# A graph layer's gather kernel: a first block without filled places, its list loaded first, and the fillers' columns computed with one partition for each step

## The chip, the cores and the metric

The kernel runs on one core of a Trainium2 chip. The metric is device time in microseconds (us), the median of three runs. Engine names follow the profile: PE is the matrix engine, PEld its weight load, DVE the vector engine, ACT the scalar engine, POOL the GpSimd engine, SP the engine that here only issues transfers. A name with a q behind it (SPq, ACTq, POOLq) is that engine's issuing side.

## The reference, cut to what matters

There are 50,000 nodes with 128 features and 1,650,000 edges, sorted by the node that they go to. Every edge carries a type, 0 or 1, which chooses one of two weight matrices.

```python
Xs  = X[src]
msg = where(edge_type == 0, Xs @ W_data.T + b_data, Xs @ W_control.T + b_control)
agg = segment_sum(msg, dst, num_segments=50000)
y   = relu(agg + X @ W_self.T + b_self)
out = layernorm(X + y)          # over the 128 features
```

The kernel uses that the sum over edges and the product with the weights can change places: it first sums the rows `X[src]` of all edges of one type that go to one node, and multiplies the sums afterwards.

## The kernel before, in words

**Blocks, chunks and steps.** The edges are cut, in their order, into 438 blocks (`NBLK`) of `BE` = 3768. A block has four steps (`Q`). A step has seven chunks (`R`) of 128 edges, and 22 fillers (`F`) behind them; after the four steps come 96 single edges (`X`). So a block has 28 chunks in its list, 88 fillers and 96 single edges. Each chunk is one indirect gather, issued by POOL at line 408: a list of 128 node numbers on the partitions brings in 128 rows of `x` as a tile `y`. There are 70 such tiles (`gat`, `bufs=70`). PE multiplies each `y` by a one-hot matrix `oh` (line 411), which puts every row into the column of its node and type. One step's nodes span at most 36 columns (`W`) for each type.

**Filled places.** Some edges in the list go from a node to itself. Their rows need no gather, because the window of `x` that a block works on is loaded anyway. `fill(b)` takes such a place in the list of chunks and puts a filler's source there instead: the number of the place among its partition's free places (`rk`) is compared with 0 to 21 (line 273), the filler's packed value is picked (lines 276 to 285) and the place's list entry `idx` comes out at line 284. The self edges that were put out are added in another way: `left_out_columns`, `left_out_matrix`, `left_out_numbers`, `left_out_rows`, `add_left_out` (lines 292 to 329). The last block has no fillers; its list comes straight from the loaded edges.

**Groups.** Ten blocks are a group (`GB`); there are 44. `load_edges(g)` brings a group's sources, targets and types on the SP queue: `s`, `d`, `t` for the chunks (128 partitions x 290 numbers, 145 KB each), and `sf`, `df`, `tf` for the fillers, where all 880 numbers of the group are copied to each of the 128 partitions (440 KB each). `columns(g)` turns them into what `fill` and `onehot` need: `col`, `rk`, `cb`, `stay` for the chunks, and `v_f`, the packed value of every filler. Both halves go through the same helpers, `columns_of`, `check` and `packed` (lines 188 to 206), and a name with `_f` marks the fillers' half. `columns(g)` is called by `fill` for the first block of a group, and `fill` runs five blocks ahead (`RAHEAD`), so that it comes in step 2 of the sixth block of the group before; `load_edges(g + 1)` is called at the second block of a group.

**Single edges.** The 96 single rows of a block are brought by plain transfers of one row each, 48 on the SP queue and 48 on the ACT queue (line 396), two blocks ahead.

**Order.** The main part stands in a hand-written order. Ahead of the loop it does `fill` for five blocks with all of the chunks' and fillers' columns, `onehot` and `counts` for two, then the windows of `x` for three and the single rows of two. In the loop, block `b` has four turns, one for each step: `products` (the gathers and matrix products), `layer` and `moments` and `store` for the block before, `onehot` and `counts` for block `b + 2`, `fill` for block `b + 5`. What stands ahead of the hand-written part (constants, the loading and transposing of the weights in a pool `wts` that is closed before the pool `keep` is opened, the load of `first_i` at line 125, `base` and `begin` at lines 127 to 135) is interleaved by the framework.

## Time and profile before

| what | value |
|---|---|
| median of three runs | 15436.6 us (15436.29 to 15437.57) |
| the profiled execution's own time | 15434.21 us |
| its span, first to last instruction | 15432.5 us |
| busy: PE / PEld / DVE / ACT / POOL | 62% / 48% / 46% / 2% / 75% |
| gathers, POOL, line 408 | 12,236 from `idx` and 27 from `s`, mean 948 ns |
| DMA moved | 1009 MB, mean 65 GB/s |

The page gives each engine's busy share, the chain of work that ended last, and the costliest groups of instructions. The view of waits says for each engine and line whom it waited for, in total, how often and the longest. The timeline lists single instructions: start in us, duration in us, engine, line, operation, output and inputs, and in brackets the idle time ahead of it with the releaser. The groups by form separate shapes: output, inputs, count, then total busy us and mean ns of one.

### The profile page before, as it was taken

What the parts mean: (1) busy time and instruction counts of PE and PEld (TensorE: products, weight loads), DVE (VectorE), ACT (ScalarE), POOL (GpSimd) and SP (SyncE); (2) the same over time, 40 slices, a digit from 0 to 9 for tenths busy, and PEclk for the clock granted to TensorE, in tenths of its full rate; (3) what the DMA queues carried; (4) which work ended last, traced back from release to release, by engine and by line L of the source; (5) the groups of instructions that cost most, each with busy time, mean ns of one, the idle gap of its engine ahead of it and who ended that gap; (6) DMA issues with size and microseconds to landing.
All of it is one profiled execution on the core that took longest, in us unless ns stands there. A gap on an engine that the chain in (4) does not pass through costs nothing.

```text
span 15432.5 us, 254222 instructions
## 1 busy us (share of the span) xinstructions
PE 9551.6 (62%) x34515; PEld 7418.5 (48%) x34516; DVE 7169.3 (46%) x12518; ACT 355.9 (2%) x881; POOL 11631.9 (75%) x12273
## 2 busy tenths in 40 slices
PE   5666666666666666666666666666666666666666
PEld 4444444444444444444444444444444444444444
DVE  5444444444444444444444444444444444444442
ACT  0000000000000000000000000000000000000000
POOL 6777777777777777777777777777777777777777
DMA  2222222222222222222222222222222222222221
GB/s 67 65 65 69 65 65 65 64 65 65 65 65 67 68 65 65 65 65 65 65 65 65 70 65 65 65 65 65 65 65 65 65 70 65 65 65 65 65 65 57
DMA packets 705933, 1008.97 MB, mean 65 GB/s; under 512 B 263521, under 2 KB 490948, under 8 KB 704222
## 3 DMA queue, kind: packets, MB, share of 16 engines
q0 software_dynamic: 392416, 804.42, 18.3%
q1 hardware_dynamic: 269416, 177.18, 4.0%
q10 hardware_dynamic: 42390, 11.02, 0.3%
q14 instruction: 1426, 11.68, 0.2%
q8 instruction: 285, 4.67, 0.1%
HBM read 962.86 MB, written 28.70 MB: 64 GB/s over the span
## 4 chain that ended last, share of the span: by engine, by line
DMA 69%; issue 11%; POOL 10%; PE 7%; DVE 2%; POOLq 0%; SPq 0%; ACTq 0%; DVEq 0%; ACT 0%
DMA y<-in_x,idx 68%; POOL y L408 10%; PE acc L411 4%; PE po L435 1%; PE po L433 1%; PE po L432 0%; POOLq L408 0%; DMA yx<-in_x 0%; SPq L396 0%; ACTq L396 0%; DVE by L292 0%; PE acc L414 0%; DMA y<-in_x,s 0%; DVE stats L198 0%; DVE stats L199 0%
## 5 line engine op out<-in xcount | busy, mean ns | idle before, releaser
L408 POOL DMA_INDIRECT y<-in_x,idx x12236 | 11605.0, 948 | 3760.9 <-DMA y<-in_x,idx 1973.1
L411 PE MATMUL acc<-oh,y 128*128 128x72 f32 x24526 | 8011.2, 446 | 5293.3 <-DMA y<-in_x,idx 5204.0
L411 PEld LDWEIGHTS acc<-oh,y 128*128 128x128 f32 x24526 | 6050.7, 315 | 7176.0 <-DMA y<-in_x,idx 6659.5
L422 DVE TENSOR_TENSOR sums<-acc,sums 128x108 f32 x1752 | 473.5, 270 | 4399.2 <-PE acc L414 4321.4
L370 DVE TENSOR_REDUCE cnt<-oh 128x216 bf16<-128x1512 f32 x438 | 1238.3, 2827 | 0.1
L360 DVE TENSOR_TENSOR oh<-col,small 128x2088 f32<-128x2088 f32 x438 | 1005.8, 2296 | 0.0
L329 DVE TENSOR_TENSOR sums<-pl,sums 128x384 f32<-128x384 f32 x437 | 243.5, 557 | 1522.8 <-ACT sums L427 1522.8
L414 PEld LDWEIGHTS <-to_row 128*128 128x128 bf16 x3504 | 639.0, 198 | 0.1
L292 DVE TENSOR_REDUCE by<-old 128x88 bf16<-128x616 f32 x437 | 583.2, 1335 | 15.1
L306 DVE COPY at<-small 88x1 f32<-88x1 f32 x437 | 67.5, 154 | 1097.9 <-PE small L299 1083.9
L440 DVE SCALAR_TENSOR_TENSOR h<-po,xw 128x128 f32<-128x128 f32 x438 | 127.5, 291 | 939.1 <-PE po L435 929.7
L435 PE MATMUL po<-wmsgT,sums 128*128 128x128 f32 x1752 | 535.3, 461 | 0.0
L375 DVE TENSOR_REDUCE cnt<-oh 128x72 bf16<-128x576 f32 x438 | 512.7, 1170 | 0.0
L427 ACT COPY sums<-sums 128x384 f32 x437 | 223.9, 512 | 12101.5 <-DMA yx<-in_x 8363.0
L414 PE MATMUL acc<-cnt,to_row 128*128 128x36 bf16 x3504 | 468.9, 217 | 0.0
L435 PEld LDWEIGHTS po<-wmsgT,sums 128*128 128x128 f32 x1752 | 406.1, 322 | 98.3 <-issue 98.3
L299 PE MATMUL small<-ones_b,by 128*88 128x1 bf16 x437 | 94.1, 215 | 493.6 <-DVE by L292 493.6
L276 DVE TENSOR_TENSOR new<-m,small 128x616 f32<-128x616 f32 x437 | 347.5, 795 | 14.9
L273 DVE TENSOR_TENSOR m<-rk,small 128x616 f32<-128x616 f32 x437 | 347.5, 795 | 14.8
L280 DVE TENSOR_REDUCE v_new<-new 128x28 f32<-128x616 f32 x437 | 347.3, 795 | 14.9
L433 PE MATMUL po<-bias,sums 3*128 3x128 f32 x876 | 346.9, 497 | 0.0
L289 DVE TENSOR_TENSOR old<-m,small 128x616 f32<-128x616 f32 x437 | 343.5, 786 | 0.1
(110 smaller groups left out, 3996.0 us busy)
## 6 DMA issues: line engine op xcount, KB each, us to landing
yx<-in_x ACTq DMA_DIRECT2D x20976, 0.5 KB
yx<-in_x SPq DMA_DIRECT2D x20976, 0.5 KB
y<-in_x,idx POOLq DMA_INDIRECT x12236
xw<-in_x SPq DMA_DIRECT2D x438, 64.0 KB
xT<-in_x_t SPq DMA_DIRECT2D x438, 64.0 KB
out<-o SPq DMA_DIRECT2D x438, 64.0 KB
sf<-in_src_f SPq DMA_DIRECT2D x44, 440.0 KB
df<-in_dst_f SPq DMA_DIRECT2D x44, 440.0 KB
```

Source lines behind the costliest of these rows:

```text
L273: nc.vector.tensor_tensor(m, rk_g[g][:, i, :, None].to_broadcast([P, C, F]), rank_no_ps[:, None, :].to_broadcast([P, C, F]), op=ALU.is_equal)
L276: nc.vector.tensor_tensor(new.rearrange("p (q r) f -> p q r f", r=R), m.rearrange("p (q r) f -> p q r f", r=R), vf.rearrange("p (q f) -> p ...
L292: nc.vector.tensor_reduce(by, old.rearrange("p (q r) f -> p q f r", r=R), AX.X, ALU.add)
L360: nc.vector.tensor_tensor(oh[:, :n, :], col_g[g][:, i, :n, None].to_broadcast([P, n, 2 * W]), num_ps[:, None, :].to_broadcast([P, n, 2 * W ...
L370: nc.vector.tensor_reduce(cnt[:, :n, :], ohs[b][:, :n * R, :].rearrange("p (q r) w -> p q w r", r=R), AX.X, ALU.add)
L375: nc.vector.tensor_reduce(cnt[:, q, :], ohs[b][:, k[0]:k[-1] + 1, :].rearrange("p r w -> p w r"), AX.X, ALU.add)
L408: nc.gpsimd.indirect_dma_start(out=y[:r], out_offset=None, in_=x, in_offset=bass.IndirectOffsetOnAxis(ap=idxs[b][:r, k:k + 1], axis=0))
L411: nc.tensor.matmul(acc[:, :2, :].rearrange("p t w -> p (t w)"), y[:r], ohs[b][:r, k, :], start=k == ks[0], stop=k == ks[-1])
L414: nc.tensor.matmul(acc[:, 2, :], to_row[:, t, :], cnts[b][:, q, t * W:(t + 1) * W], start=t == 0, stop=t == 1)
L422: nc.vector.tensor_tensor(part, accs.pop((b, q)), part, op=ALU.add)
L433: nc.tensor.matmul(po, a[0:3, 2, :B], bias, start=False, stop=False)
L435: nc.tensor.matmul(po, a[:, t, :B], c["wmsgT"][:, t * D:(t + 1) * D], start=False, stop=t == 1)
```

## The change

**Block 0 is plain.** It gets 28 chunks of 128 edges and neither fillers nor single edges, like the last block. `plain(b)` is true for the first and the last block; `fill`, the five `left_out` functions and `single_rows` skip them. Its list is a tile of its own, `idx0`, 128 x 28 numbers, loaded on the SP queue ahead of the first `load_edges`. The number of blocks stays 438; the last block gets 28 chunks (3568 edges) in place of 27 (3384).

**The fillers' half on the partitions of its steps.** `sf`, `df`, `tf` become tiles of 40 x 22: one partition for each of the group's 40 steps, one column for each filler, loaded as they lie. The fillers' `rel`, `col`, `chk`, `lim` and `v` are 40 x 22 too, with their start `begin_p` computed once for all groups from a small load `first_p`. The result, 880 numbers, is written to a DRAM tile (`spread_out`) and read back to all 128 partitions (`spread_in`, tile `vf_all`, 440 KB), both on the SP queue.

**The order.** `load_edges(g + 1)` moves to the first block of a group, `columns(g + 1)` out of `fill` to step 2 of the third block, ahead of `left_out_rows`; `spread_out(g + 1)` and `spread_in(g + 1)` stand at the heads of the fourth and fifth. Ahead of the loop come the columns of group 0, the two transfers, the windows, `onehot` and `counts` of block 0, and then blocks 1 to 4 one after another.

```diff
-NBLK = -(-E // BE)
-REST = E - (NBLK - 1) * BE
+NBLK = 2 + (E - C * CH) // BE
+REST = E - C * CH - (NBLK - 2) * BE
...
+GS = GB * Q
+def plain(b):
+    return b == 0 or b >= NBLK - 1
...
+    nc.vector.memset(stats, 0.0)
...
         for name, a in (("sf", src_f), ("df", dst_f), ("tf", etype_f)):
-            t = eds.tile([P, GB, Q, F], I32, name=name, bufs=1)
-            nc.sync.dma_start(t.rearrange("p b q f -> p (b q f)"),
-                              row_bcast(a[g * GB * Q * F:(g + 1) * GB * Q * F]))
+            t = eds.tile([GS, F], I32, name=name, bufs=1)
+            nc.sync.dma_start(t, a[g * GS:(g + 1) * GS, :])
...
+    idx0 = keep.tile([P, C], I32, name="idx0")
+    nc.sync.dma_start(idx0, src_t[:, :C])
     load_edges(0)
...
+    two_p = keep.tile([GS, 2, GROUPS], I32, name="two_p")
+    nc.sync.dma_start(two_p, first_p.rearrange("s (m g) -> s m g", m=2))
+    base_p = keep.tile([GS, GROUPS], F32, name="base_p")
+    nc.vector.tensor_scalar(base_p, two_p[:, 1, :], 0.0, float(N - B), op0=ALU.max, op1=ALU.min)
+    begin_p = keep.tile([GS, GROUPS], F32, name="begin_p")
+    nc.vector.tensor_tensor(begin_p, two_p[:, 0, :], base_p, op=ALU.subtract)
+    nc.vector.tensor_scalar(begin_p, begin_p, 0.0, float(B - W), op0=ALU.max, op1=ALU.min)
+    nc.vector.tensor_tensor(begin_p, begin_p, base_p, op=ALU.add)
...
-            yield rel, d, first[:, :, :, None].to_broadcast([P, GB, Q, F])
+            yield rel, d, begin_p[:, g:g + 1].to_broadcast([GS, F])
...
+    def spread_out(g):
+        vd_g[g] = dram.tile([GS * F], F32, name="vd")
+        nc.sync.dma_start(vd_g[g].rearrange("(s f) -> s f", f=F), vp_g.pop(g))
+    def spread_in(g):
+        v = eds.tile([P, GB, Q, F], F32, name="vf_all")
+        nc.sync.dma_start(v.rearrange("p b q f -> p (b q f)"), row_bcast(vd_g.pop(g)))
+        v_g[g] = v
     def fill(b):
+        if plain(b):
+            return
         g, i = divmod(b, GB)
-        if i == 0:
-            columns(g)
...
-        nc.vector.tensor_copy(vf, v_f[:, i].rearrange("p q f -> p (q f)"))
+        nc.vector.tensor_copy(vf, v_g[g][:, i].rearrange("p q f -> p (q f)"))
...
-        n = C1 if b < NBLK - 1 else RCH if b < NBLK else 0
+        n = C1 if not plain(b) else C if b == 0 else RCH if b < NBLK else 0
...
-    idxs, bys, pcs, zs, pls = {}, {}, {}, {}, {}
+    idxs = {0: idx0}
+    bys, pcs, zs, pls = {}, {}, {}, {}
...
     with tc.manual_schedule():
-        for b in range(RAHEAD):
+        columns(0)
+        spread_out(0)
+        spread_in(0)
+        for b in range(3):
+            window(b)
+        onehot(0)
+        counts(0)
+        for b in range(1, RAHEAD):
             fill(b)
             left_out_columns(b)
             left_out_matrix(b)
-        for b in range(AHEAD):
-            onehot(b)
-            counts(b)
-        for b in range(3):
-            window(b)
-        for b in range(AHEAD):
-            for q in range(Q):
-                single_rows(b, q)
-        left_out_numbers(0)
-        left_out_rows(0)
+            if b < AHEAD:
+                onehot(b)
+                counts(b)
+                for q in range(Q):
+                    single_rows(b, q)
         for b in range(NBLK + 1):
             if b + 3 < NBLK:
                 window(b + 3)
             g, i = divmod(b, GB)
-            if i == 1 and g + 1 < GROUPS:
+            if i == 0 and g + 1 < GROUPS:
                 load_edges(g + 1)
+            if i == 3 and g + 1 < GROUPS:
+                spread_out(g + 1)
+            if i == 4 and g + 1 < GROUPS:
+                spread_in(g + 1)
...
+                if q == 2 and i == 2 and g + 1 < GROUPS:
+                    columns(g + 1)
                 if q == 2:
                     left_out_rows(b + 1)
                     if b + RAHEAD < NBLK:
                         fill(b + RAHEAD)
...
-                if b + AHEAD < NBLK - 1:
+                if not plain(b + AHEAD):
                     single_rows(b + AHEAD, q)
```

The host's layout of the edge lists follows these shapes.

More of the change, by code (lines that the diff above doesn't have):

```diff
@@ L65, with straight @@
 TBL = GROUPS * GB
+GS = GB * Q
+def plain(b):
+    return b == 0 or b >= NBLK - 1
 def row_bcast(ap, n=P):
     return bass.AP(tensor=ap.tensor, offset=ap.offset, ap=[[0, n], *ap.ap])
-def straight(ctx, tc, c, x, x_t, src_t, dst_t, etype_t, src_f, dst_f, etype_f, src_x, dst_first, out):
+def straight(ctx, tc, c, x, x_t, src_t, dst_t, etype_t, src_f, dst_f, etype_f, src_x, dst_first, first_p, out):
     nc = tc.nc
@@ L88, in straight @@
     keep_ps = ctx.enter_context(tc.tile_pool(name="keep_ps", bufs=1, space=bass.MemoryType.PSUM))
+    dram = ctx.enter_context(tc.tile_pool(name="vdram", bufs=2, space=bass.MemoryType.DRAM))
     eds = ctx.enter_context(tc.tile_pool(name="eds", bufs=2))
@@ L99, in straight @@
     loads = {}
-    col_g, rk_g, v_g, cb_g, one_g = {}, {}, {}, {}, {}
+    col_g, rk_g, stay_g, v_g, cb_g, vp_g, vd_g = {}, {}, {}, {}, {}, {}, {}
     stats = keep.tile([P, 2, 2, GROUPS], F32, name="stats")
+    nc.vector.memset(stats, 0.0)
     loops = keep.tile([P, GROUPS], F32, name="loops")
@@ L196, in check @@
         nc.vector.scalar_tensor_tensor(chk, d, float(DST_PAD), rel, op0=ALU.is_lt, op1=ALU.mult)
-        axes = AX.XY if len(d.shape) == 3 else AX.XYZ
+        axes = AX.XY if len(d.shape) == 3 else AX.X
         nc.vector.tensor_reduce(at[0], chk, axes, ALU.min)
@@ L238, in columns @@
         col_f, rel_f = columns_of(a["df"], a["tf"], first_of_f, "_f")
-        check(a["df"], rel_f, [stats[:, 1, m, g:g + 1] for m in range(2)], "_f")
+        check(a["df"], rel_f, [stats[:GS, 1, m, g:g + 1] for m in range(2)], "_f")
         v = packed(a["s"], col, "")
@@ L252, in columns @@
                                        op0=ALU.mult, op1=ALU.add)
+        at = Q if g == 0 else 0
         n = (min((g + 1) * GB, NBLK - 1) - g * GB) * Q
-        nc.vector.tensor_reduce(loops[:, g:g + 1], rank[:, :n, R:], AX.XY, ALU.min)
+        nc.vector.tensor_reduce(loops[:, g:g + 1], rank[:, at:n, R:], AX.XY, ALU.min)
         stay = eds.tile([P, GB, C], F32, name="stay")
         nc.vector.scalar_tensor_tensor(stay, rk, F - LOOP, v[:, :, :C], op0=ALU.is_ge, op1=ALU.mult)
-        col_g[g], rk_g[g], v_g[g], cb_g[g], one_g[g] = col, rk, (stay, v_f), cb, a
+        col_g[g], rk_g[g], stay_g[g], cb_g[g], vp_g[g] = col, rk, stay, cb, v_f
+        if g == GROUPS - 1:
+            idxs[NBLK - 1] = a["s"][:, NBLK - 1 - g * GB, :]
+    def spread_out(g):
[5 more added lines that the diff above has]
+        v_g[g] = v
     def fill(b):
+        if plain(b):
+            return
         g, i = divmod(b, GB)
-        if i == 0:
-            columns(g)
-        if b == NBLK - 1:
-            idxs[b] = one_g[g]["s"][:, i, :]
-            return
-        stay, v_f = v_g[g]
         two = lists[b % 2]
         vf, cb = two[:, :Q * F], two[:, Q * F:]
-        nc.vector.tensor_copy(vf, v_f[:, i].rearrange("p q f -> p (q f)"))
+        nc.vector.tensor_copy(vf, v_g[g][:, i].rearrange("p q f -> p (q f)"))
         nc.vector.tensor_copy(cb, cb_g[g][:, i, :])
@@ L281, in fill @@
         vi = fil.tile([P, C], I32, name="vi")
-        nc.vector.tensor_tensor(vi, v, stay[:, i, :], op=ALU.add)
+        nc.vector.tensor_tensor(vi, v, stay_g[g][:, i, :], op=ALU.add)
         idx = fil.tile([P, C], I32, name="idx", bufs=RAHEAD + 2)
@@ L295, in left_out_columns @@
     def left_out_columns(b):
-        if b < NBLK - 1:
+        if not plain(b):
             pc = sums_at[b % 2]
@@ L302, in left_out_matrix @@
     def left_out_matrix(b):
-        if b < NBLK - 1:
+        if not plain(b):
             z = fil.tile([Q * F, 2, P], BF16, name="z", bufs=RAHEAD + 1)
@@ L310, in left_out_numbers @@
     def left_out_numbers(b):
-        if b < NBLK - 1:
+        if not plain(b):
             z = zs.pop(b)
@@ L321, in left_out_rows @@
     def left_out_rows(b):
-        if b < NBLK - 1:
+        if not plain(b):
             rows = pls[b][:, :2, :B]
@@ L326, in add_left_out @@
     def add_left_out(b):
-        if b < NBLK - 1:
+        if not plain(b):
             part = sums[b % RING][:, :, :B]
@@ L357, in onehot @@
         g, i = divmod(b, GB)
-        n = C1 if b < NBLK - 1 else RCH
+        n = C1 if not plain(b) else C if b == 0 else RCH
         oh = ohp.tile([P, C1, 2 * W], F32, name="oh")
@@ L776, in gnn_resnorm @@
     dst_first: bass.AP,
+    first_p: bass.AP,
     src: bass.AP,
@@ L815, in gnn_resnorm @@
         straight(own, tc, c, x, x_t, src_t, dst_t, etype_t, src_f, dst_f, etype_f, src_x,
-                 dst_first, out)
+                 dst_first, first_p, out)
     found = nc.values_load(bad, min_val=0, max_val=4 * P,
@@ L832 @@
         arrays[k] = np.pad(a, (0, EPAD - E), constant_values=pad)
-        a = np.pad(a, (0, TBL * BE - E), constant_values=pad).reshape(TBL, BE)
+        n = C * CH
         step = R * CH + F
-        steps = a[:, :Q * step].reshape(TBL, Q, step)
+        a = np.pad(a, (0, n + (TBL - 1) * BE - E), constant_values=pad)
+        rest = a[n:].reshape(TBL - 1, BE)
+        steps = rest[:, :Q * step].reshape(TBL - 1, Q, step)
         cols = np.full((TBL, C1 * CH), pad, np.int32)
-        cols[:, :C * CH] = steps[:, :, :R * CH].reshape(TBL, C * CH)
-        cols[:, C * CH:C * CH + X] = a[:, Q * step:]
-        fills = np.ascontiguousarray(steps[:, :, R * CH:])
-        firsts = steps[:, :, 0].copy()
-        cols[NBLK - 1] = a[NBLK - 1, :C1 * CH]
-        fills[NBLK - 1] = pad
-        firsts[NBLK - 1] = a[NBLK - 1, [q * R * CH for q in range(Q)]]
+        cols[0, :n] = a[:n]
+        cols[1:, :n] = steps[:, :, :R * CH].reshape(TBL - 1, n)
+        cols[1:, n:n + X] = rest[:, Q * step:]
+        cols[NBLK - 1, :n] = rest[NBLK - 2, :n]
+        cols[NBLK - 1, n:] = pad
+        fills = np.full((TBL, Q, F), pad, np.int32)
+        fills[1:NBLK - 1] = steps[:NBLK - 2, :, R * CH:]
+        ones = np.full((TBL, X), pad, np.int32)
+        ones[1:] = rest[:, Q * step:]
+        firsts = np.ascontiguousarray(cols[:, [q * R * CH for q in range(Q)]])
         arrays[k + "_t"] = np.ascontiguousarray(cols.reshape(TBL * C1, CH).T)
-        arrays[k + "_f"] = fills.reshape(-1)
+        arrays[k + "_f"] = fills.reshape(TBL * Q, F)
         if k == "src":
-            arrays["src_x"] = np.ascontiguousarray(a[:, Q * step:].reshape(-1))
+            arrays["src_x"] = ones.reshape(-1)
         if k == "dst":
-            arrays["dst_first"] = np.ascontiguousarray(firsts.reshape(-1))
+            arrays["dst_first"] = firsts.reshape(-1)
+            both = np.stack([firsts, np.repeat(firsts[:, :1], Q, 1)]).reshape(2, GROUPS, GS)
+            arrays["first_p"] = np.ascontiguousarray(both.transpose(2, 0, 1).reshape(GS, 2 * GROUPS))
     arrays["x_t"] = np.ascontiguousarray(arrays["x"].T)
@@ L859 @@
         gnn_resnorm(tc, ap["x"], ap["x_t"], ap["src_t"], ap["dst_t"], ap["edge_type_2_t"], ap["src_f"], ap["dst_f"],
-                    ap["edge_type_2_f"], ap["src_x"], ap["dst_first"], ap["src"],
+                    ap["edge_type_2_f"], ap["src_x"], ap["dst_first"], ap["first_p"], ap["src"],
                     ap["dst"], ap["edge_type_2"],
```

## The prediction

> **What bounds the kernel now.** I read the page first: no engine is full, POOL is the busiest, and its time is one line.

> ```profile
> PE 9551.6 (62%) x34515; PEld 7418.5 (48%) x34516; DVE 7169.3 (46%) x12518; ACT 355.9 (2%) x881; POOL 11631.9 (75%) x12273
> L408 POOL DMA_INDIRECT y<-in_x,idx x12236 | 11605.0, 948 | 3760.9 <-DMA y<-in_x,idx 1973.1
> ```

> The reader is to see 3760.9 us of idle time beside 12,236 gathers: 0.307 us for each. Whether that is waiting or the price of an issue, the view of waits tells.

> ```profile
> POOL y L408 <- DMA y<-in_x,idx: 1973.7, 6469, 0.3
> POOL y L408 <- issue: 1361.7, 4464, 0.3
> POOL y L408 <- DVE idx L284: 28.2, 1, 28.2
> ```

> The longest of 6469 is 0.3 us, as long as those with no releaser ("issue"), so 0.3 us belongs to every gather. POOL waited once, 28.2 us, for the first list. After that it never stops: PE, at 62%, follows it. The kernel's time is POOL's start, the row of gathers, and a tail. The timeline gives start and end.

> ```profile
> 5.49 0.46 ACTq L806 DMA_DIRECT2D w_sb<-in_L_gnn_W_self  x1
> 12.38 0.33 SPq L125 DMA_DIRECT2D first_i<-in_dst_first  x1
> 12.42 0.20 POOL L146 IOTA num<- 128x72 f32 x1 [11.02 <-PE pw L808]
> 41.67 1.15 POOL L408 DMA_INDIRECT y<-in_x,idx  x1 [28.24 <-DVE idx L284]
> ...
> 15412.06 0.92 POOL L408 DMA_INDIRECT y<-in_x,s  x1 [0.30 <-issue]
> ```

> From 41.67 to 15412.06 lie 12,262 spacings, 1.2535 us each in the mean. Reading all POOL rows, nearly all spacings are 1.24 or 1.25: blocks away from group heads give 1.2486. That makes 15310.3 us; 60.1 us are left. They lie almost wholly in the two blocks of each group around `columns`, 1.37 us for each of 43 groups (59 us). So the span is 41.7 + 15310.3 + 60.1 + 20.4 (tail) = 15432.5 us. What stretches gathers there, the timeline of one group's columns shows.

> ```profile
> 246.77 0.30 DVE L190 TENSOR_SCALAR col<-t 128x290 f32<-128x290 int32 x1
> 246.80 1.09 POOL L408 DMA_INDIRECT y<-in_x,idx  x1 [0.30 <-DMA y<-in_x,idx]
> 248.71 1.06 DVE L188 TENSOR_TENSOR rel_f<-df,begin 128x880 f32<-128x880 int32 x1
> 249.44 1.15 POOL L408 DMA_INDIRECT y<-in_x,idx  x1 [0.30 <-DMA y<-in_x,idx]
> 250.34 1.08 DVE L191 TENSOR_TENSOR col_f<-col_f,rel_f 128x880 f32<-128x880 f32 x1
> 250.89 1.33 POOL L408 DMA_INDIRECT y<-in_x,idx  x1 [0.30 <-DMA y<-in_x,idx]
> 254.91 0.46 DVE L206 SCALAR_TENSOR_TENSOR v<-s,lim 128x290 f32<-128x290 int32 x1
> 255.04 1.14 POOL L408 DMA_INDIRECT y<-in_x,idx  x1 [0.30 <-PE acc L414]
> 255.93 1.08 DVE L206 SCALAR_TENSOR_TENSOR v_f<-sf,lim_f 128x880 f32<-128x880 int32 x1
> 256.49 1.33 POOL L408 DMA_INDIRECT y<-in_x,idx  x1 [0.30 <-issue]
> ```

> One rule, mine, fits all of this group's gathers: 0.14 us after its start a gather stands still if a DVE operation with two SBUF inputs, or a fast one-input one (880 numbers in 0.61 us), is running, until that one ends. 250.89 + 0.14 = 251.03, `col_f` ends at 251.42: 0.39, and the gather takes 1.33 in place of 0.94. Reductions and operations with an input in PSUM don't do it. Of the 1.34 us here, 0.99 are the fillers' rows.

> **The change, part by part.**

> *First gather.* It no longer needs `columns` and `fill`, only `idx0`. But `num`, `first_i` and the others in `keep` all began at 12.4, after the last weight's transpose, which had waited for a load issued at 5.49 that landed 6.3 us later. `idx0` lies in `keep` too, so I take it to wait for the same. The two weights before took 1.9 and 2.7 us; the last one shared the queues with 1.3 MB of fillers' copies, which are gone. With 2.5 us it lands at 8.0, its transpose ends at 8.5, `idx0` (14 KB) lands 2 us later: first gather at 10.5. From 6.5 (no wait) to 14.6 (last weight as late as before).

> *Block 0's own stretches.* Its gathers now run beside the preparation. Operations of length L that hold POOL cost L squared over 2.5 in the mean: the two `begin` rows (1.92 and 1.97) 3.0, two of 1.06 us 0.9, the smaller ones and `columns` 1.1. I take 5 us, from 2 to 8.

> *One more gather.* 438 x 28 = 12,264 in place of 12,263: 1.25 us.

> *Is block 1's list there in time?* It is due when 28 gathers are out: 10.5 + 35 + 5 = 50.5. `first_i` took at most 4.4 us, so `base` can begin at 13.3, 3.5 earlier; `begin_p` and the new memset cost five small operations, 1.0. Columns begin at 22.3 instead of 24.8. The eight fillers' operations took 7.2 us, and at 22 numbers on 40 partitions I give them 1.3 (128x28 takes 0.19, some overlapped). `v_f` is there at 27.4, the columns end at 29.5. The trip through DRAM: the small write 2.0 (as a weight), the 440 KB read 3.2 (between 1.9 for 64 KB and 4.4 for 880 KB): 32.6. Behind `spread_out` on SP stand `spread_in`, three windows and block 1's rows, none due before 85. DVE does `onehot(0)` and `counts(0)` until 35.7, then 3.4 us of `fill(1)`: list at 39.1, 11 us to spare. The trip costs nothing because these two cover it; without the cover its 5.2 us would come on top, and the list would still be 6 us early.

> *The y tiles.* PE can't begin before the `fill` of block 4 (its `left_out_columns` stand ahead of `products`). By the spacings of the prologue's rows (rest of a `fill` 3.2, one-hot and counts 6.3, a whole `fill` 6.55) DVE gets there at 39.1 + 3.2 + 6.3 + 3 x 6.55 = 68; 42 gathers are out by then, of 70 tiles. No stop.

> *The columns in the loop.* DVE loses 5.9 us for each group; DVE is not the bound, this alone is worth nothing. What counts are the stretches. The fillers' 0.99 us falls to nearly nothing, but the chain moves against the gathers: it begins right after `add`, 0.45 us earlier. Laying the chain with the rule above, `h_loop` now meets a gather (0.30), which shifts the next into `chk` (0.29), and the small ones or `cb` take 0.05 to 0.4. I take 0.85 for 1.37, 43 x 0.52 = 22 us saved; bounds 0.35 and 1.2. With the few stretches elsewhere 37.5 us are left of 60.1.

> [...]

> *SP, ACT, and the rest at nothing.* The filler loads shrink from 1.3 MB to 10 KB a group, two transfers come in, 96 single rows (24 us of issuing on each queue) go. They lie beside the gathers, which need neither; SP's own waits sum to some 3300 us, so it is busy 28 of 35 us a block. `spread_out` waits for `v_f`: behind it stand window, rows and `store`. SP issues `out` at 253.77 for an `o` computed at 236.70, so it comes 17 us behind DVE and finds `v_f` done. If not, PE's lag is covered by 70 tiles, 87 us. `columns` two blocks after their load instead of four: still 70 us. The tail stays.

> **The sum.** 10.5 + 12,263 x 1.2486 (15311.6) + 5 + 37.5 + 20.4 = 15385.0 us of span. Own time is 1.7 above the span (15434.2), the median 2.4 above that: 15389, 47 us or 0.3% under the time before.

> **The rivals.**

> *The stretches only move.* The chain keeps 1.37 us a group by meeting gathers elsewhere. For it: `h_loop` and `chk` are set to collide. Against: the long rows are gone. 15389 + 43 x 0.52 = 15411.

> *The early start is eaten.* Block 1's list comes late, or the y tiles run out, and POOL waits out what it gained: 15389 + 26 = 15415. Against it: 11 us to spare and 28 tiles free. Or `idx0` is not really first: then 14.6 for 10.5, 15393, inside my range.

> *SP becomes the bound.* This one ends slower. If SP stood at the two spread transfers for more than its slack, 10 x 6.4 = 64 us a group, single rows would come late, PE would stop in order, the tiles would fill and POOL would stop; each us beyond costs 43. At 66 us a group it passes 0.2% above the old time, near 15470. The 17 us by which SP trails DVE speaks against it.

> **How the numbers follow.** Both gains hold: 0.80, alone 15361 (start at 6.5, 2 us, 0.35 a group) to 15411 (14.6, 8, 1.2). Stretches move: 0.08. Start eaten: 0.07. SP bound: 0.05. What 0.2% is (31 us), about the least that a measurement of this kernel can tell from no change, ends at 15405.7. Of the first case nearly all lies under it, of the second a quarter: faster 0.80, same 0.14, slower 0.06. The range is the first case's own, 15360 to 15411, which nearly takes in the second.

> **What would show it.** Right: the first gather between 6 and 15, no POOL wait over 0.5 us after it, 1.25 spacings, no 1.33 rows beside fillers, 0.35 to 1.2 us a group. Wrong: a long POOL wait for `idx` of block 1 or for PE; stretches of 1.3 us a group; SP later than DVE's `v_f` by blocks.

## The result, and the profile after

| | before | after |
|---|---|---|
| median of five runs | 15436.6 us | 15355.11 us (15353.54 to 15357.15) |
| span of the profiled execution | 15432.5 us | 15353.4 us |
| first gather starts | 41.67 us | 9.65 us |
| gathers | 12,263 | 12,264 |

The ratio is 0.9947, with a 95% interval of 0.9933 to 0.9961. The change saves 81.5 us. The forecast was 47 us, 15389, with a range from 15360 to 15411: the direction was right, and the time lies 5 us below the range.

The page after, its head and its costliest line:

```profile
PE 9635.8 (63%) x34511; PEld 7437.8 (48%) x34512; DVE 6897.0 (45%) x12507; ACT 356.1 (2%) x881; POOL 11584.5 (75%) x12274
L436 POOL DMA_INDIRECT y<-in_x,idx x12236 | 11556.6, 944 | 3733.2 <-issue 2519.6
```

The reader is to see the mean of one gather: 944 ns for 948 before. Four ns times 12,236 are about 49 us, and they are most of the gain. The idle time is 3733.2 for 3760.9; the 28.2 us of the first wait have gone. In the view of waits, all that is left of POOL's waiting at this line is its own 0.3 us (columns: us in total, times, longest):

```profile
POOL y L436 <- issue: 2526.9, 8283, 0.3
POOL y L436 <- PE acc L439: 577.2, 1892, 0.3
POOL y L436 <- DMA y<-in_x,idx: 419.9, 1376, 0.3
```

POOL still sets the time, from its first gather to its last, and neither block 1's list nor a free `y` tile ever made it wait. The timeline of the preparation, after:

```profile
5.20 0.37 ACTq L843 DMA_DIRECT2D w_sb<-in_L_gnn_W_self  x1
7.14 0.45 PE L845 MATMUL pw<-ident,w_sb 128*128 128x128 f32 x1 [2.65 <-DMA w_sb<-in_L_gnn_W_self]
7.62 0.35 SPq L129 DMA_DIRECT2D idx<-in_src_t  x1
9.65 1.12 POOL L436 DMA_INDIRECT y<-in_x,idx  x1 [0.62 <-DMA idx<-in_src_t]
...
26.20 0.30 SPq L282 DMA_DIRECT2D vd<-v_f  x1
27.49 0.35 SPq L287 DMA_DIRECT2D vf_all<-vd  x1
34.03 0.24 DVE L297 COPY small<-vf_all 128x88 f32<-128x88 f32 x1
...
37.24 0.18 DVE L311 TENSOR_SCALAR idx<-vi 128x28 int32<-128x28 int32 x1
```

The last weight takes 1.9 us in place of 6.3. `idx0` (the profile calls it `idx`) is issued once the transpose is done, and lands 2 us later. The small write to DRAM is followed 1.3 us later by the read back, and DVE takes `vf_all` as soon as it has finished `counts(0)`. Block 1's list is there at 37.4.

And one group's columns in the loop, in the timeline:

```profile
461.85 0.94 POOL L436 DMA_INDIRECT y<-in_x,idx  x1 [0.30 <-DMA y<-in_x,idx]
461.99 0.45 DVE L245 TENSOR_TENSOR h_loop<-s,d 128x280 bf16<-128x280 int32 x1
463.10 0.94 POOL L436 DMA_INDIRECT y<-in_x,idx  x1 [0.30 <-issue]
463.14 0.46 DVE L209 TENSOR_TENSOR col<-col,rel 128x290 f32<-128x290 f32 x1
...
465.50 0.29 DVE L222 TENSOR_SCALAR lim<-col 128x290 f32<-128x290 f32 x1
465.60 1.01 POOL L436 DMA_INDIRECT y<-in_x,idx  x1 [0.31 <-PE acc L439]
```

The long fillers' rows are gone, and with them the gathers of 1.33 us. But look at 461.85 and 463.10: an operation with two SBUF inputs begins 0.14 and 0.04 us after the gather has started, is still running 0.14 us into it, and the gather takes its plain 0.94. The rule that the prediction drew from the trace of before says that both stand still. Only the gather at 465.60, which started when `lim` was already running, is longer, by 0.07.

### The profile page after: what moved, and what is told of

Same layout as the page of the kernel before. It is cut to its first block, busy times and chain, and to the rows that moved or that the text cites. A ratio compares the mean times of both kernels' runs of the same rounds, so it can differ in the third digit from the quotient of the medians.

```text
span 15353.4 us, 253982 instructions
## 1 busy us (share of the span) xinstructions
PE 9635.8 (63%) x34511; PEld 7437.8 (48%) x34512; DVE 6897.0 (45%) x12507; ACT 356.1 (2%) x881; POOL 11584.5 (75%) x12274
## 4 chain that ended last, share of the span: by engine, by line
DMA 39%; issue 33%; PE 15%; POOL 7%; DVE 4%; SPq 1%; ACTq 1%; POOLq 0%; DVEq 0%; ACT 0%
DMA y<-in_x,idx 38%; PE acc L439 9%; POOL y L436 7%; PE po L463 2%; PE po L461 1%; PE po L460 1%; DMA yx<-in_x 1%; SPq L424 1%; ACTq L424 1%; DVE by L319 0%; PE acc L442 0%; DVE new L303 0%; DVE m L300 0%; DVE v_new L307 0%; DVE old L316 0%
## 5 line engine op out<-in xcount | busy, mean ns | idle before, releaser
L436 POOL DMA_INDIRECT y<-in_x,idx x12236 | 11556.6, 944 | 3733.2 <-issue 2519.6
L398 DVE TENSOR_REDUCE cnt<-oh 128x216 bf16<-128x1512 f32 (+1 forms) x438 | 1240.8, 2833 | 0.1
L388 DVE TENSOR_TENSOR oh<-col,small 128x2088 f32<-128x2088 f32 (+1 forms) x438 | 1005.7, 2296 | 0.0
L460 PE MATMUL po<-wselfT,xT 128*128 128x128 f32 x876 | 340.1, 492 | 0.0
```

The lines of the kernel that those rows point to most:

```text
L388: nc.vector.tensor_tensor(oh[:, :n, :], col_g[g][:, i, :n, None].to_broadcast([P, n, 2 * W]), num_ps[:, None, :].to_broadcast([P, n, 2 * W ...
L398: nc.vector.tensor_reduce(cnt[:, :n, :], ohs[b][:, :n * R, :].rearrange("p (q r) w -> p q w r", r=R), AX.X, ALU.add)
L436: nc.gpsimd.indirect_dma_start(out=y[:r], out_offset=None, in_=x, in_offset=bass.IndirectOffsetOnAxis(ap=idxs[b][:r, k:k + 1], axis=0))
L460: nc.tensor.matmul(po, xTs.pop(b), c["wselfT"], start=True, stop=False)
```

## The experiments

The experiments are to tell two rules apart. The **moment rule** is the prediction's: a gather stands still if an operation with two SBUF inputs, or a fast one-input one, is running 0.14 us after it started. The **start rule** came out of the trace after: it is held only if such an operation is already running when it starts, until that operation ends, less 0.12 us.

The record names chips 7, 5 and 8 for the experiments, and no chip for the two kernels above; I call theirs the first chip. On the three the kernel before took 22,260, 22,081 and 22,092 us in place of 15,437. So none of their times bears on the 81 us; how long single gathers took, and when the first began, can still be read. The last part of this section shows what is slower there.

**The parts alone, and the columns later.** Front only: the fillers go back to 128 partitions and copied loads, the rest of the change stays.

```diff
-            t = eds.tile([GS, F], I32, name=name, bufs=1)
-            nc.sync.dma_start(t, a[g * GS:(g + 1) * GS, :])
+            t = eds.tile([P, GB, Q, F], I32, name=name, bufs=1)
+            nc.sync.dma_start(t.rearrange("p b q f -> p (b q f)"),
+                              row_bcast(a[g * GS:(g + 1) * GS, :].rearrange("s f -> (s f)")))
...
-        spread_out(0)
-        spread_in(0)
...
```

> The changed kernel with one part undone: the fillers' columns are again computed on 128 partitions from copied loads, without the DRAM trip; the plain first block, its early list and the new order stay. Both theories: first gather near 14.4 us (the last weight shares the queues with the copies again). Start rule (a gather is held only by a two-input or fast DVE operation that is already running when it starts): laying the long rows into the new order gives 1.4 us of stretch a group, 15353.4 + 5 + 3 + 43 x 1.26 = about 15415 us of span. Moment rule (the one of the prediction: what counts is what runs 0.14 us after the start): 2.2 us a group, about 15448.

Fillers only: the kernel before with `sf`, `df`, `tf` on 40 partitions, `spread_out`, `spread_in` and the new places of loads and columns in the loop, and its own front:

```diff
     with tc.manual_schedule():
+        columns(0)
+        spread_out(0)
+        spread_in(0)
         for b in range(RAHEAD):
             fill(b)
...
```

> The kernel before with one part done: the fillers' columns on 40 partitions, spread by way of DRAM, in the new order of loads and columns in the loop; the first block stays filled and the gathers begin after fill of block 0. Both: the first gather moves from 41.7 to about 35, because the loads shrink, the long fillers' rows go, and the DRAM trip comes in. Start rule: 0.17 us a group, so 15436 - 7 - 43 x 1.2 = about 15378 us. Moment rule: 0.85 us a group, about 15407.

The changed kernel with the columns pushed back by a memset of 1060 or of 110 numbers:

```diff
                 if q == 2 and i == 2 and g + 1 < GROUPS:
+                    nc.vector.memset(pause[:, :1060], 0.0)
                     columns(g + 1)
```

> The changed kernel with a memset of 128 x 1060 numbers (about 1.0 us, one output, no input) ahead of the columns in the loop, so that the chain of columns meets the gathers 1.0 us later. Start rule: the stretches rise from 0.17 to about 0.7 us a group, 23 us more, near 15378. Moment rule: 0.74 in place of 0.90, that is no more than before the shift; near 15350. If the stretches come from the amount of DVE work and not from where it falls: unchanged, 15355.

> The same with a memset of 128 x 110 numbers, 0.13 to 0.16 us. Start rule: stretches fall to about 0.09 us a group, 15351. Moment rule: about 0.5 us a group, 15370.

Measured. Stretch is what gathers took over 0.943 us, of those over by more than 0.03; per group it is the sum behind block 0 over 43 groups:

| kernel | time, us | ratio to before on that chip | first gather | stretch, block 0 | stretch per group |
|---|---|---|---|---|---|
| before (first chip) | 15436.6 | | 41.67 | 0.3 | 1.38 |
| after (first chip) | 15355.1 | 0.9947 | 9.65 | 3.8 | 0.17 |
| front only | 22233 | 0.9989 (0.9979 to 0.9998) | 14.40 | 8.2 | 1.18 |
| fillers only | 22378 | 1.0052 (1.0036 to 1.0069) | 34.12 | 0.3 | 0.19 |
| columns 1.0 us later | 22266 | 1.0000 (0.9990 to 1.0010) | 9.32 | 5.0 | 0.46 |
| columns 0.13 us later | 22259 | one run | 9.39 | 3.9 | 0.23 |

The first gathers came where the edits put them: 14.4 with the fillers' copies still in the queues, 34 without them and with the first block filled. The stretches go with the fillers' rows: 1.18 with them, 0.19 without, and the moment rule's 2.2 and 0.85 are met in neither. The two pushed-back kernels decide nothing by their shift alone. Where POOL is stopped by other things, its gathers meet the columns at any moment, and a shift by a known time has no known effect; that 1.0 us later is dearer (0.46) points the start rule's way, but its 0.7 was worked out for the other case. Why the fillers alone came out 0.5% slower there stays open.

**The kind of operation.** Eight extra rows behind each group's columns, on tiles that nothing else uses:

```diff
                     columns(g + 1)
+                    for _ in range(8):
+                        nc.vector.tensor_tensor(more[2], more[0], more[1], op=ALU.add)
```

> The changed kernel with eight extra DVE operations behind the columns of each group in the loop, each adding two SBUF tiles of 128 x 880 (about 1.07 us). Nothing uses them. If operations with two SBUF inputs hold the gathers: start rule 2.2 us more a group, 93 us, near 15448; moment rule 3.5 us more a group, near 15505. If only the fast one-input rows hold them: 15355, no stretch beside the extra rows.

The same with `tensor_reduce(more[2][:, 0:1], more[0], AX.X, ALU.add)`:

> The same with eight reductions of one SBUF tile of 128 x 880 (about 1.07 us each) in the place of the additions. If the kind of operation counts: no stretch beside them, near 15355. If the length of the DVE work counts: as with the additions, near 15448.

And with `tensor_scalar(more[2], more[0], 0.0, 1.0, op0=ALU.max, op1=ALU.min)`:

> The same with eight one-input tensor_scalar operations on 128 x 880 numbers in SBUF (0.61 us each, the fast form). [...]

The times were 22104, 22141 and 22188 us, one run each, beside 22081 (22020 to 22119) for before: nothing can be read from them. The gathers were stretched by 1.40 us a group with the additions, by 0.16 with the reductions, by 0.40 with the fast rows (1.24, 0.00 and 0.20 of it beside the extra rows). Additions and reductions take the same time, 1075 and 1070 ns (median), and of the two only the additions held POOL. A fast row took 619 ns, from 605 to 805. The timeline of the first group with additions:

```profile
223.97 8.86 DVE L544 TENSOR_TENSOR more<-more,more 128x880 f32<-128x880 f32 x8
224.33 1.52 POOL L439 DMA_INDIRECT y<-in_x,idx  x1 [0.30 <-issue]
226.16 0.94 POOL L439 DMA_INDIRECT y<-in_x,idx  x1 [0.30 <-remote]
227.40 1.79 POOL L439 DMA_INDIRECT y<-in_x,idx  x1 [0.30 <-issue]
229.50 0.95 POOL L439 DMA_INDIRECT y<-in_x,idx  x1 [0.30 <-issue]
230.75 1.78 POOL L439 DMA_INDIRECT y<-in_x,idx  x1 [0.30 <-issue]
```

Eight additions run without a pause, and yet every second gather is plain. A held gather is released when an addition ends, so the next one starts some 1.14 us later, just as another addition begins; it goes free, and the one after starts 1.25 us on and runs into one again. The 2.2 us that was expected by the start rule was worked out for a full stream of gathers; laid over the starts that gathers and additions really had, the rule gives 1.25 us a group, and 1.24 were measured.

**The rules, counted.** All fourteen traces can be asked. A gather behind block 0 is a trial if exactly one operation of the kinds below, on more than 200 numbers, runs between its start and 0.14 us later, and has at least 0.24 us to go at the start. Stretched means longer than 0.973 us.

| operation | when | before and after: stretched | the twelve experiments: stretched |
|---|---|---|---|
| two SBUF inputs | running 0.03 us or more before the gather starts | 192 of 196 | 775 of 784 |
| two SBUF inputs | begins 0.03 to 0.14 us after the start | 0 of 33 | 5 of 30 |
| one input, fast | running 0.03 us or more before the start | 20 of 20 | 72 of 72 |
| one input, fast | begins 0.03 to under 0.12 us after the start | none | 37 of 37 |
| one input, fast | begins 0.12 to 0.14 us after the start | 0 of 3 | 0 of 23 |
| reduction | running 0.03 us or more before the start | 0 of 4220 | 0 of 15,296 |

For two inputs the start rule holds: the second row is where the rules differ, and there 58 of 63 gathers went free. The other five all stand in the kernel with the fast rows, where a fast row began 0.47 us into the gather. The 13 exceptions in the first row began within 0.05 us ahead of the gather, and took 0.52 to 0.54 us in place of 0.45, and the gather was not stretched; there it was DVE's operation that took longer. For fast one-input rows the start rule fails, and the moment rule holds, with 0.12 us for its moment: they held gathers that started first (37 of 37). The length of a hold, to the end of the operation less 0.12 us, agrees within 0.05 us in 1018 of the 1072 trials that were already running. An operation with one input in SBUF and one in PSUM, running 0.03 us or more before the start, stretched none in the traces of before and after: 0 of 1889.

The two together, laid over each trace's own starts, give 0.22 us a group for the kernel after (0.17 measured), 1.50 for before (1.38), and 0.46 and 0.23 for the two pushed-back kernels (0.46 and 0.23).

**The list ahead of the weights.** `idx0` in the pool opened first, its load the first on SP, and the short memset ahead of the columns:

```diff
+    idx0 = const.tile([P, C], I32, name="idx0")
+    nc.sync.dma_start(idx0, src_t[:, :C])
     ident = const.tile([P, P], F32, name="ident")
```

> The changed kernel with the first block's list in the pool that is opened ahead of the weights', its load the first on SP, and the memset of 128 x 110 ahead of the columns. First gather near 3.5 us in place of 9.65, so 6 us less, and 43 x 0.08 = 3 us less of stretch: near 15346. POOL makes its constants after eleven gathers, so DVE gets num and rank_no near 17 us; if that delays block 1's list beyond 40 us, POOL waits and the gain is smaller or gone, 15350 to 15360.

The first gather came at 3.02 us, 6.6 before the one after the change; 5.6 us of stretch in block 0 in place of 3.8 take 1.8 of it back. The delay that the expectation named came too: block 1's list was there only at 45.6 us, and POOL waited for it.

```profile
45.85 0.94 POOL L436 DMA_INDIRECT y<-in_x,idx  x1 [2.01 <-DVE idx L311]
```

With POOL's constants between the gathers this takes another 2.3 us. Block 1's first gather came at 45.85 us, after 48.44 in the kernel after: 2.6 us are left of the 6.6. The time was 22096 us, ratio 1.0007 (0.9998 to 1.0015), which can't show so little.

**Half the single rows.** To make the gathers the bound on every chip, I set `X = 48` in four kernels.

```diff
-X = 96
+X = 48
```

> The kernel before with X = 48 single edges a block in place of 96, nothing else. It computes the same; the blocks get smaller, 444 in place of 438, with 12,420 gathers, and the ACT and SP queues issue 24 rows each a block. On the chips of the first eight runs a row costs a queue about 1 us and the single rows, not the gathers, set the time; with half of them the gathers should set it on every chip. Both theories: 41.7 + 12,419 x 1.2487 + 44 x 1.37 + 20.5 = about 15630 us of span, with gather spacings of 1.25.

> The changed kernel with X = 48. First gather near 9.5, 12,421 gathers. Start rule (a gather is held only by a two-input or fast DVE operation that is already running when it starts): 0.17 us a group as in the trace of after, about 15550 us, 80 under the one before. Moment rule (the prediction's): 0.85 us a group, about 15580.

> X = 48, with the front alone changed: plain first block, early list, new order, and the fillers' columns on 128 partitions from copied loads. First gather near 14.4, 8 us of stretch in the first block. Start rule: 1.2 to 1.45 us a group (1.18 was read in the first run of this edit, where the gathers were not the bound), 15605 to 15615 us. Moment rule: 2.2 us a group, 15648.

> X = 48, with the fillers alone changed: 40 partitions, DRAM trip, new place of the columns, and the first block filled as before. First gather near 34. Start rule: 0.17 us a group, about 15570 us. Moment rule: 0.85, about 15600. If front and fillers add up, x3 and x4 together save what x2 saves, but for the 5 us by which the smaller loads bring the front forward, which both contain in part.

| kernel, X = 48 | median, us | ratio to before (X = 96) on that chip | first gather | stretch per group (44) |
|---|---|---|---|---|
| before | 18485 | 0.8375 (0.8358 to 0.8392) | 42.80 | 1.71 |
| front only | 18368 | 0.8318 (0.8304 to 0.8332) | 15.43 | 1.63 |
| fillers only | 18261 | 0.8268 (0.8255 to 0.8282) | 37.26 | 0.38 |
| after | 18224 | 0.8257 (0.8240 to 0.8274) | 11.80 | 0.38 |

The expectation of 15,550 to 15,630 us failed by 17 to 18%: the gathers were still not the bound. The stretches split as before, again by the fillers alone. The change saves 261 us here, the fillers alone 224, the front alone 117, so the two don't add up. The fillers' 224 are nearly four times the 59 us that 44 x 1.33 us of stretch account for, so something else gains there as well.

What the other chips are short of, the view of one line's instructions shows, first of the kernel after, then of front only (columns: shortest/median/longest ns):

```profile
L424 ACTq FUSED_REGOPS  x20928: 37/37/37, 3.6 to 15237.3; - x200
L424 SPq FUSED_REGOPS  x20928: 37/37/42, 33.2 to 15233.8; - x200
```

```profile
L417 ACTq FUSED_REGOPS  x20928: 2/37/1421, 3.4 to 22148.9; - x200
L417 SPq FUSED_REGOPS  x20928: 2/37/1426, 25.4 to 22145.7; - x200
```

A register operation that takes 37 to 42 ns on the first chip takes up to 1426 there, and its median is the same. So issuing comes in fits, on both queues that bring single rows. The fuller one is SP. Summed over the view of its waits, it waits 3292 of 15353 us in the kernel after, and 627 of 22,206 us in front only; the rest, its issuing with every fit in it, grew from 12.1 to 21.6 ms. ACT, DVE and POOL end up behind the rows (view of waits, front only):

```profile
ACT sums L448 <- DMA yx<-in_x: 17950.9, 370, 60.7
DVE sums L349 <- ACT sums L448: 12127.9, 410, 41.1
POOL y L429 <- PE acc L432: 5565.0, 1332, 18.6
```

With `X = 48` it is plainer. ACT's queue stood still, in stretches of over 2 us, for 4.8 to 5.1 ms, SP's for 0.1 to 0.8 ms. SP waited 752 us in before, 681 in front only, 573 in fillers only and 531 in after, and what is left of the four spans is the same, 17,665 to 17,697 us. So these kernels differ by SP's waits, and most of what the fillers gain is one of them, the wait at the store for `o` (before, then fillers only):

```profile
SPq L455 <- DVE o L454: 253.2, 39, 17.1
SPq L472 <- DVE o L471: 62.0, 14, 13.9
```

Of the 253 us, 168 lie right behind the columns, in 12 of the 44 groups (front only: 136 us in 15); with the fillers' rows short, 17 us are left there, in 3. So DVE's long rows keep SP standing at its store, and SP has no time to spare; how they come to delay `o` by some 14 us at a time is open. That SP's issuing sets the time is read from these sums; no run took work from SP alone. Why instructions come late on those chips was not settled.

## Why the prediction was wrong, by its own steps

| step | forecast, us | measured, us |
|---|---|---|
| first gather | 10.5 | 9.65 |
| stretch in block 0 | 5 | 3.8 |
| 12,263 plain spacings | 15311.6 | 15312.0, at 1.24864 |
| stretches elsewhere | 37.5 | 7.4 |
| tail | 20.4 | 20.6 |
| span | 15385.0 | 15353.4 |
| median over span | 4.1 | 1.7 |

**What bounds it, right.** The sum of start, spacings, stretches and tail closes on the span in both traces; of its terms one was mis-sized.

**First gather, right.** `idx0` did wait for the weights' pool, and the last weight landed 1.9 us after its issue (2.5 taken) once the copies were gone. Front only confirmed the reason: with the copies back, 14.4, against the prediction's bound of 14.6.

**Block 0, one more gather, block 1's list, the y tiles: right.** The stretch in block 0 was 3.8 for 5. The list was due at 48.4 for 50.5, and was there at 37.4 for 39.1. The DRAM trip was covered as the forecast said.

**The columns in the loop, wrong in size.** "I take 0.85 for 1.37": it was 0.17, under the lower bound of 0.35 too, read as the two blocks around the columns less what every block has. Times 43, that is 29 of the 32 us by which the span was missed. The step that failed is "Laying the chain with the rule above, `h_loop` now meets a gather (0.30), which shifts the next into `chk` (0.29)". In 30 of the 43 groups `h_loop` began up to 0.14 us after a gather had started, so that it ran at the moment that counts in the prediction's rule. The moment rule makes that the dearest place, the start rule makes it free, and it was free: none of the 30 gathers was stretched, and `chk` stretched none either. The rule had fitted all eleven gathers of the group that it was read from, because there every operation that held a gather was already running when the gather started; the two rules gave the same answer wherever I looked. The start rule, laid over the after trace's own starts, gives 0.2 us a group, and the moment rule about 0.8. So the rule was wrong for two SBUF inputs, on which most of this term rested; for fast one-input rows, by the count above, it was right.

**The rivals.** None came on the first chip. The stretches did not move, POOL never waited for a list or a tile, and SP still waited 3292 us. On the other three SP was full, as the third rival has it, and POOL stopped behind PE; but the prediction priced a wait at the spread transfers, and there it was the issuing itself.

**What is shown and what is argued.** That the fillers' long rows caused the stretches is shown by taking them out alone, twice. The split into parts is a sum over the two traces of the first chip, whose spans differ by 79 us: 32 us of earlier start, less 1.25 for one more gather and 3.5 of stretch in block 0, and 52 us of stretches. The medians differ by 81.5, since the trace of before is of a run 2.4 us under its median. No run with the parts alone was timed where the gathers set the time.

**A better version.** On chip 8, `X = 48` with the change takes 17% less than the kernel before; the kernel after was not run there. On the first chip `X = 48` was not run; its 157 more gathers would cost 196 us there at 1.2486 each, an estimate. The list ahead of the weights should give about 2.6 us there, also an estimate, from its start of block 1.

## What to carry to other kernels

Where one engine issues a steady row of the same instruction, take the time as start, count times plain spacing, and stretches, and look for what runs beside the stretched ones; four ns of a mean were 49 us here. A rule drawn from a trace has to be tried on the cases where a neighbouring rule would answer otherwise, here operations that begin just after the gather; with none of those in sight, both answers belong in the range. What hides a cost on one chip, here the queue of SP with 7.5 us to spare in a block (3292 us over 438 blocks), need not hide it on the next.
